# Context attention in a transformer block: one output tile, the regrouping of score blocks and the order of two half weighings are moved

## The chip, the cores and the metric

The kernel runs on 1 core of one Trainium2 chip. The metric is device time in microseconds (us) of one execution. A core has five engines with instruction streams of their own: TensorE (PE, matmuls; PEld its weight loads), VectorE (DVE), ScalarE (ACT), GpSimd (POOL) and SyncE (SP, which here issues almost all DMAs). Each executes its stream in the order in which it was written; semaphores tie them together.

## What is computed

One transformer block in float32 on x of 2 x 1024 x 256 with a context of 2 x 154 x 192: self attention, context ("cross") attention, and a gated feed-forward part, each behind a layer norm and with a residual.

```python
h = _layernorm(x, ln1_g, ln1_b)
x = _attention(h, h, sa_wq, sa_wk, sa_wv, sa_wo, sa_bo) + x
h = _layernorm(x, ln2_g, ln2_b)
x = _attention(h, cond_emb, ca_wq, ca_wk, ca_wv, ca_wo, ca_bo) + x
h = _layernorm(x, ln3_g, ln3_b)
p = h @ ff_w1 + ff_b1
a, gate = (p[..., :D_FF], p[..., D_FF:])
h = a * jax.nn.gelu(gate, approximate=False) @ ff_w2 + ff_b2
return h + x
```

Both attentions have 16 heads of 64; softmax runs over 1024 keys in the first and over 154 in the second.

## The kernel before

The order of all instructions is written out by hand (`manual_schedule`): every engine gets its instructions in the order in which the Python code emits them.

The work is cut into 16 units (2 batches x 8 pairs of heads). Three loops follow each other: self attention (to about 700 us), context attention (48 groups `c`, about 700 to 903 us), and the gated part (steps `k`, from there to the end). In context attention a unit has three groups, of 3, 3 and 2 tiles of 128 queries; group `c` belongs to unit `ui = c // 3` and has the place `n = c % 3` in it.

A unit `u` of context attention passes these stations:

- its query weights are loaded by DMA (L134, `ca_wq`) at group 3(u-2)+1, its queries are projected (`cross_queries`, `pq_ca`, two banks of PSUM) at group 3(u-1), and ScalarE copies them out (L381, `q_ca`);
- at groups 3u to 3u+2 its scores are made (`cross_first`, `sc`, L828), VectorE takes their maximum (`neg`, L834), ScalarE the exponents (L845), VectorE the reciprocals (`rden`, L853) and GpSimd scales (L856);
- two groups later each group is transposed by VectorE (`cross_turn`, L872) into one of three rings `pT_ca`; the last of a unit at group 3u+4;
- `cross_regroup` (L889) copies the blocks from the ring with eight DMAs of 128 KB into one buffer `pTc["pairs"]` (named `wf` in the trace), so that two blocks stand on the partitions that one matmul wants. There is one such buffer for all units: the blocks of unit u may be written only when those of unit u-1 have been read;
- at group 3u+7 `cross_weigh` runs `cross_values` (`poc`, L908) for two halves: half 0 in two banks of the pool `sum_tile` (two banks in all) and half 1 in two banks of the pool `mm_tile` (two banks in all). VectorE copies the four results to `o_ca` (L922); in the gated part ScalarE takes two of the four;
- `out_piece` (L471, `py`) multiplies by the output weights, and VectorE adds the result to x (L478).

Every second unit's values (`context_values`, `pv_ca`, L788) are projected at place 1 of an even unit; their weights (L123, `ca_wv`) are loaded one unit before at place 2. The values are spread over partitions by two DMAs (L800) and four more (L805), which stand in the list `later`. Each group ends with `cross_regroup(c)` and then two entries of `later`; ff weights (L968, L971) and the output weights `ca_wo` (L1287) stand in that list too.

At place 1 of a unit the code runs, in this order: one step of the next layer norm (`side`, through `run_work(0, 1, ...)`), one output tile in a `sum_tile` bank, the values, one output tile in an `mm_tile` bank (`run_work(1, 0)`), the pending additions to x (`flush(adds)`), and `cross_weigh`. The last four output tiles of self attention are put in the list at group 5; two run there, and two at group 7. A step of the layer norm runs only when the tiles that it reads have been added.

In the gated part step `k` counts on as c = 48 + k. Units 14 and 15 are weighed there, at k = 1 and k = 5. `gate_first` takes an `mm_tile` bank (`pa`) and two of another pool; `gate_second` ends with `Gelu` on it (L1066).

Of the kernel before, what the change touches and what calls it, by code (L numbers as in the profile page):

```python
# [18 lines left out]
def tile_transformer_block(ctx: ExitStack, tc: tile.TileContext, a: dict, out: bass.AP):  # L19
# [11 lines left out]
    HP = NPAIR // NQ  # L31
# [182 lines left out]
    hT, vs, qk, oT = {}, {}, {}, {}  # L214
# [347 lines left out]
    def run(piece):  # L562
        done = piece()
        if done is not None:
            (adds if getattr(done, "adds", False) else stores).append(done)

    def flush(queue):
        for fn in queue:
            fn()
        queue.clear()  # L570

    def run_work(n, n_side, bank=None, n_sum=0):

        while n > 0 and work:
            n -= work[0].banks
            run(work.pop(0))
        for _ in range(min(n_side, len(side))):  # L580
            needs_bank, needs, fn = side[0]
            if needs_bank and not bank and n <= 0 or not added.issuperset(needs):
                break
            if needs_bank and not bank:
                n -= 1
            spare["bank"] = bank or mm_tile
            run(fn)
            side.pop(0)
        for i in range(min(max(n, 0) + n_sum, len(outs))):
            spare["out"] = mm_tile if i < n else sum_tile  # L590
            run(outs.pop(0))
# [139 lines left out]
    CG = [(t, min(TG, NT - t)) for t in range(0, NT, TG)]  # L731
# [145 lines left out]

    def cross_regroup(c):

        ui, n = divmod(c - len(CG) - 2, len(CG))  # L880
        if n != 0 or not 0 <= ui < NU:
            return
        for a2 in range(2):
            for a4 in range(P // KB):
                half, e = divmod(a4, 2)
                own = slice(a4 * KB, (a4 + 1) * KB)
                src = slice((2 * half + a2) * KB, (2 * half + a2 + 1) * KB)
                blocks = pTc["ring"][src, ui % 3, :2 * NM].rearrange("p (m e) j q -> p m e (j q)", e=2)
                nc.sync.dma_start(  # L889
                    out=pTc["pairs"][own, a2].rearrange("p m j q -> p m (j q)"), in_=blocks[:, :, e])  # L890

    def cross_values(ui, a2):

        b, pr = units[ui]
        v, v0 = vs["ca", b, pr // 2], pr % 2 * P
        if a2 == 0 and pr % HP == 0:
            oT["ca", b, pr // HP] = pt_.tile([P, HP, S], F32, tag="oT", name=f"o_ca{b}_{pr}")  # L900
        quarters = (a2, 2 + a2)
        po = {a4: (mm_tile if a2 else sum_tile)(f"poc_{ui}_{a4}") for a4 in quarters}
        for m in range(NM + 1):
            for a4 in quarters:
                r0 = a4 // 2 * QG
                r = slice(r0, r0 + QG)
                for j in range(2):
                    nc.tensor.matmul(  # L908
                        po[a4][j * DH:(j + 1) * DH, :NT * KB],
                        lhsT=v[r, m + a2 * (m == NM), v0 + j * DH:v0 + (j + 1) * DH],  # L910
                        rhs=pTc["pairs"][r, a2, m, j] if m < NM else
                        pTc["ring"][r, ui % 3, NB - 1, j, :],
                        start=(m == 0), stop=(m == NM),
                        tile_position=(r0, j * DH),
                    )
        dst = oT["ca", b, pr // HP][:, pr % HP, :].rearrange(
            "p (t a q) -> p t a q", a=P // KB, q=KB)

        def store():
            for a4 in quarters:  # L920
                copy = nc.scalar.copy if pools and a4 // 2 else nc.vector.tensor_copy
                copy(dst[:, :, a4, :], po[a4][:, :NT * KB].rearrange("p (t q) -> p t q", q=KB))  # L922

        return store
# [12 lines left out]
    def cross_drain(c):  # L937

        n = c - 2
        if 0 <= n < CA:  # L940
            cross_turn(n)

    def cross_weigh(c):

        ui, n = divmod(c - 2 * len(CG) - 1, len(CG))
        if n == 0 and 0 <= ui < NU:
            for part in range(2):
                run(lambda: cross_values(ui, part))
            flush(stores)

# [4 lines left out]
    wsum, wh, ub, psum, pools = {}, {}, {}, {}, {}  # L955
# [156 lines left out]
    with tc.manual_schedule():  # L1112
# [59 lines left out]
        for p in range(SA):  # L1172
# [19 lines left out]
            ui, n = divmod(p, 2 * SH)  # L1192
# [8 lines left out]
            if hg == LAG:  # L1201
# [5 lines left out]
                if n == SH + LAG and ui in (0, 1, NU - 1):  # L1207

                    pr = {0: 2, 1: 4, NU - 1: 6}[ui]
# [3 lines left out]
        for c in range(CA):  # L1213
            if c == 1:
                pTc["ring"] = pt_.tile(
                    [P, 2 * NK, QH // 2], F32, tag="pT", name="pT_ca"
                ).rearrange("p a b -> p (a b)")[:, :3 * 2 * NB * NT * KB].rearrange(
                    "p (u n j q) -> p u n j q", u=3, n=NB, j=2)
            if c == SH + 1:
                out_pieces("sa", B - 1, NQ - 1, out_order("sa"))  # L1220
            if c == SH + 1:

                w1, w2, parts = hold_gated()
                add_biases("ca", 0)
                others = later[:] + [lambda: None] * (len(parts) - len(later))
                later[:] = [fn for pair in zip(parts, others) for fn in pair] + others[len(parts):]
            ui, n = divmod(c, len(CG))
            nxt = units[ui + 1] if ui + 1 < NU else None
            if n == 0:
                cross_beside(ui)  # L1230
            elif n == 1 and 1 <= ui < NU - 2:
                load_weights("ca", units[ui + 2][1], "q")
            elif n == 2 and nxt and ui:
                load_weights("ca", nxt[1], "v")
            flush(adds)
            then = cross_first(c)
            if c < 2:
                reciprocals(SA - 2 + c)
            flush(stores)
            if c == 1:  # L1240
                turn_group(SA - 2, 0)
                turn_group(SA - 2, 1)
                scale_rows(SA - 1, 0, 4)
            flush(lates)
            lates.append(then())
            if c == 0:
                join(SA - 1)
                turn_group(SA - 3, 1)
            if c == 2:
                turn_group(SA - 1, 0)  # L1250
                turn_group(SA - 1, 1)
            cross_drain(c)
            if c == 0:
                run(lambda: self_values(2 * NU - 2, 1))
            elif c == 1:
                run(lambda: cross_queries(*nxt))
            elif c == 2:
                run(lambda: cross_queries(*units[2], bank=sum_tile))
            elif c == 3:
                run(lambda: self_values(2 * NU - 1, 0))  # L1260
            elif c == 4:
                run(lambda: self_values(2 * NU - 1, 1))
            elif n == 0 and ui:
                if nxt:
                    run(lambda: cross_queries(*nxt))
                else:
                    run_work(2, 0)
                run_work(0, 1)
            elif n == 1:

                spare["turned"] = True
                run_work(0, 1, sum_tile if outs else None)
                flush(stores)
                run_work(0, 0, n_sum=1)
                if ui % 2 == 0:
                    run(lambda: context_values(*units[ui]))
                run_work(1, 0)
                flush(adds)
                flush(stores)
                cross_weigh(c)  # L1280
            elif n == 2:
                run_work(0, 1, sum_tile if ui == HP + 1 else None)
                if c == SH + 1:
                    run_work(2, 0)
                elif ui == HP:
                    wo["ca"] = const.tile([P, NPAIR, D], F32, tag="wo", name="ca_wo")
                    later[:0] = [lambda i=i: nc.sync.dma_start(  # L1287
                        out=wo["ca"][:, i, :], in_=w["ca_wo"][i * P:(i + 1) * P, :])
                        for i in range(NPAIR)]
            cross_regroup(c)  # L1290
            for _ in range(min(2, len(later))):
                later.pop(0)()
            if c == CA - 16:
                weighted = [fn for n in range(4) for fn in weight_sums(n)]
            if CA - 16 <= c < CA - 4:
                weighted.pop(0)()
            elif c >= CA - 3:
                for n in {CA - 3: (4,), CA - 2: (5, 6), CA - 1: (7,)}[c]:
                    weight_sums(n)[0]()
            if c == CA - 5:  # L1300
                token_sums(0)
# [7 lines left out]
        for k in range(2 * FU):  # L1309
            c = CA + k  # L1310
# [59 lines left out]
```

## Time and profile before

| | |
|---|---|
| runs, median (lowest to highest) | 1085.54 us (1083.54 to 1085.69), 3 runs |
| profiled execution, its time | 1084.96 us |
| its span | 1083.2 us |
| context attention's 16 weighings (`poc`, L908) | first 736.0 us, last 924.5 us |
| regrouping transfers (L889) | 128, 128 KB each |
| granted TensorE clock | 1.00 in all stretches from 715 us on |

The span is the time between the first and the last instruction of the program. "Idle before" is the idle time of an engine just before an instruction, with what ended it behind the arrow. In the order of time, rows of equal instructions are merged: the first column is the start, the second how long they took together, and `x8` their number; `SPq` is SyncE's queue of issues. TensorE's records count each float32 matmul twice, so one weighing of both halves has 48. In the stretches' sums the columns are length, busy time of PE, PEld, DVE, ACT and POOL, granted clock, busy share of DMA, and GB/s.

### The profile page before, as it was taken

To read this page: it belongs to the slowest core of one execution; us is meant where nothing else is said; L and a number is where in the kernel's file an instruction comes from. 1 tells how busy PE (TensorE), PEld (TensorE's weight loads), DVE (VectorE), ACT (ScalarE), POOL (GpSimd) and SP (SyncE) were. 2 spreads that over 40 slices of the span, in tenths; PEclk is the share of its full clock that TensorE was granted. 3 is DMA by queue.
4 is the path that set the end of the run, shared out by engine and by line. 5 is a ranking of instruction groups with operands and counts; after the bars stand their busy time and mean duration, and the time that the engine had idled before them with its cause. 6 is when DMAs were issued, how large, how long until landed. Compare 5 with 4: busy or idle time off the path is not lost.

```text
span 1083.2 us, 46388 instructions
## 1 busy us (share of the span) xinstructions
PE 1067.0 (99%) x19156; PEld 703.2 (65%) x19156; DVE 878.7 (81%) x1297; ACT 643.5 (59%) x2062; POOL 727.1 (67%) x1552
## 2 busy tenths in 40 slices
PE   8999999999999999999999999999999999999998
PEld 6556556556565565575665655566776677788887
DVE  5799999998989989999999889968877887654442
ACT  5766666777667657666776776656555554242321
POOL 2677777777777777677777777776756785475321
PEclk9999999999999999999999999999999999999999
DMA  3222122112111121111111101136765545000000
GB/s 91 68 70 52 39 48 53 43 43 50 32 43 34 30 50 38 34 43 34 33 42 25 43 14 38 29 79 150 191 157 125 119 107 118 1 10 15 11 14 30
DMA packets 104724, 60.81 MB, mean 56 GB/s; under 512 B 32378, under 2 KB 95298, under 8 KB 104514
## 3 DMA queue, kind: packets, MB, share of 16 engines
q1 hardware_dynamic: 103138, 57.07, 22.2%
q8 instruction: 151, 2.47, 1.0%
q10 hardware_dynamic: 1376, 0.79, 0.2%
q14 instruction: 59, 0.48, 0.1%
HBM read 27.91 MB, written 2.10 MB: 28 GB/s over the span
## 4 chain that ended last, share of the span: by engine, by line
PE 83%; DVE 4%; POOL 4%; DMA 3%; SPq 2%; ACT 2%; issue 1%; POOLq 0%; DVEq 0%; ACTq 0%
PE po L549 18%; PE s L497 17%; PE py_sa L471 5%; PE pf L1095 5%; PE py_ca L471 5%; PE pk_sa L366 4%; PE pv_sa L397 4%; PE poc L908 4%; PE pq_ca L366 4%; PE pq_sa L366 4%; PE pb L1029 4%; DMA st<-st 3%; PE sc L828 2%; PE pa L1029 2%; PE pc L1029 2%; SPq L518 2%
## 5 line engine op out<-in xcount | busy, mean ns | idle before, releaser
L619 POOL TENSOR_SCALAR p<-p,rd,ee 128x512 f32<-128x512 f32 x512 | 390.4, 768 | 90.8 <-DVE rd L609 87.7
L508 ACT ACTIVATE p<-s,st 128x512 f32<-128x512 f32 x512 | 345.0, 686 | 171.1 <-DVE st L681 163.7
L681 DVE TENSOR_REDUCE st<-s 128x2 f32<-128x1024 f32 x256 | 308.5, 1206 | 56.9 <-issue 19.0
L644 DVE STREAM_TRANSPOSE pT<-p 128x1024 f32<-128x1024 f32 x256 | 302.7, 1219 | 2.4 <-POOL p L619 2.1
L497 PE MATMUL s<-k_sa,q_sa 64*32 64x512 f32 x4096 | 252.8, 591 | 3.3 <-ACT p L508 2.5
L549 PE MATMUL po<-pT,v_sa 64*32 64x256 f32 x8192 | 237.1, 376 | 1.0 <-DVE pT L644 1.0
L549 PEld LDWEIGHTS po<-pT,v_sa 64*32 64x32 f32 x8192 | 172.9, 106 | 76.2 <-issue 31.2
L497 PEld LDWEIGHTS s<-k_sa,q_sa 64*32 64x32 f32 x4096 | 78.4, 106 | 104.6 <-issue 57.6
L845 ACT ACTIVATE p<-sc,neg 128x154 f32<-128x154 f32 x256 | 96.1, 403 | 83.0 <-DVE rden L853 79.3
L856 POOL TENSOR_SCALAR p<-p,rden 128x154 f32<-128x154 f32 x256 | 96.8, 398 | 56.7 <-DVE rden L853 56.5
L508 ACT ACTIVATION_READ_ACCUMULATOR p<-s,st 128x1 f32 x512 | 103.9, 203 | 0.0
L526 POOL TENSOR_TENSOR dd<-st 128x8 f32<-128x8 f32 x128 | 25.6, 200 | 74.9 <-DMA st<-st 73.0
L397 PEld LDWEIGHTS pv_sa<-sa_wv,hT_ln 64*128 64x128 f32 x1024 | 58.5, 188 | 14.2 <-issue 8.4
L397 PE MATMUL pv_sa<-sa_wv,hT_ln 64*128 64x128 f32 x1024 | 61.8, 275 | 0.0
L471 PE MATMUL py_ca<-ca_wo,o_ca 128*128 128x256 f32 x256 | 60.0, 382 | 0.5 <-DVE o_ca L922 0.5
L366 PE MATMUL pq_ca<-hT_ln,ca_wq 64*64 64x512 f32 (+1 forms) x544 | 60.1, 590 | 0.0
L471 PE MATMUL py_sa<-sa_wo,o_sa 128*128 128x256 f32 x256 | 59.7, 385 | 0.2 <-ACT v_sa L406 0.2
L471 PEld LDWEIGHTS py_sa<-sa_wo,o_sa 128*128 128x128 f32 x256 | 47.3, 190 | 18.2 <-issue 6.9
L834 DVE TENSOR_REDUCE neg<-sc 128x6 f32<-128x924 f32 (+1 forms) x48 | 47.9, 998 | 13.7 <-PE sc L828 13.3
L366 PE MATMUL pq_sa<-hT_ln,sa_wq 64*32 64x512 f32 (+1 forms) x976 | 56.6, 586 | 0.0
L366 PE MATMUL pk_sa<-hT_ln,sa_wk 64*32 64x512 f32 x960 | 56.2, 590 | 0.3 <-ACT q_sa L381 0.3
L845 ACT ACTIVATION_READ_ACCUMULATOR p<-sc,neg 128x1 f32 x256 | 56.1, 219 | 0.0
(121 smaller groups left out, 1418.9 us busy)
## 6 DMA issues: line engine op xcount, KB each, us to landing
wf<-pT_ca SPq DMA_DIRECT2D x128, 128.0 KB
st<-st SPq DMA_DIRECT2D x512, 1.0 KB
v_sa<-v_sa SPq DMA_DIRECT2D x32, 256.0 KB
sa_wq<-in_L_xattn_sa_wq_dram SPq DMA_DIRECT2D x32, 128.0 KB
sa_wk<-in_L_xattn_sa_wk_dram SPq DMA_DIRECT2D x32, 128.0 KB
sa_wv<-in_L_xattn_sa_wv_dram SPq DMA_DIRECT2D x32, 128.0 KB
ca_wq<-in_L_xattn_ca_wq_dram SPq DMA_DIRECT2D x32, 128.0 KB
wf<-in_L_xattn_ff_w_dram SPq DMA_DIRECT2D x12, 256.0 KB
```

The lines of the kernel that those rows point to most:

```text
L366: nc.tensor.matmul(pq[r][f:f + m, at:at + n], lhsT=wt[own, c, f:f + m], rhs=h[own, c, t0:t0 + n], start=(c == 0), stop=(c == NH - 1), tile ...
L397: nc.tensor.matmul(pv[r][:, i * P:(i + 1) * P], lhsT=h[own, c, i * P:(i + 1) * P], rhs=wt[own, c, :], start=(c == 0), stop=(c == NH - 1), ...
L471: nc.tensor.matmul(py[:, e * D:(e + 1) * D], lhsT=o[:, i, (t + e) * P:(t + e + 1) * P], rhs=wo[kind][:, g * HP + i, :], start=(i == 0), st ...
L497: nc.tensor.matmul(sc[a4 * KB:(a4 + 1) * KB, j, :], lhsT=q[r, c:c + KB], rhs=k[r, h * HB:(h + 1) * HB], start=True, stop=True, tile_positi ...
L508: nc.scalar.activation(pr[:, j, :], sc[:, j, :], AF.Exp, bias=st[:, 0, 0, i, j:j + 1], accum_out=st[:, 0, 1, i, j:j + 1],)
L549: nc.tensor.matmul(po[a2][d:d + KB, :QH // 2], lhsT=v[r, t, e, d:d + KB], rhs=pT[r, d // DH * NK + n, :], start=(t == 0 and e == 0), stop= ...
L619: nc.gpsimd.tensor_scalar(pr[:, j, :], pr[:, j, :], own["rd"][:, c:c + 1], own["ee"][:, 0, c:c + 1], op0=ALU.mult, op1=ALU.mult,)
L644: nc.vector.transpose(halves[h][:, :, c:c + KB], slots[p]["p"][i].rearrange("p j (n k) -> p (j n) k", k=KB))
L681: nc.vector.tensor_reduce(st[:, 0, 0, i, :], sc[i], AX.X, ALU.max, negate=True)
L845: nc.scalar.activation(pr_[:, j, i, :T], sc[:, j, i * T:(i + 1) * T], AF.Exp, bias=neg[:, j, i:i + 1], accum_out=den[:, j, i:i + 1],)
L856: nc.gpsimd.tensor_scalar(pr_[:, j, i, :T], pr_[:, j, i, :T], rden[:, j, i:i + 1], 1.0, op0=ALU.mult, op1=ALU.mult,)
L1029: nc.tensor.matmul(into[:, :BT], lhsT=lhs, rhs=wh[pair][i], start=first, stop=True, skip_group_check=True)
```

## The change

Four edits:

- `cross_regroup` runs for unit u at group 3u+4 instead of 3u+5, except for unit 0, which stays at group 5. At group 3u+4 it stands behind the weighing of unit u-1 and ahead of that group's two entries of `later`. For units 14 and 15 this is group 46 and step k = 1.
- At group 7 the second output tile of place 1 (`run_work(1, 0)`) is left out. It is the last entry of the list, and is run at group 10 as the tile in the `sum_tile` bank. At group 10 one more step of the layer norm runs behind the additions.
- In the gated part (`pools` is filled there) half 1 of a weighing comes before half 0.
- The tile for a pair's outputs is made when it is first needed, whichever half comes first.

```diff
     def cross_regroup(c):

-        ui, n = divmod(c - len(CG) - 2, len(CG))
+        ui, n = divmod(c - len(CG) - (2 if c < 2 * len(CG) else 1), len(CG))
...
-        if a2 == 0 and pr % HP == 0:
+        if ("ca", b, pr // HP) not in oT:
             oT["ca", b, pr // HP] = pt_.tile([P, HP, S], F32, tag="oT", name=f"o_ca{b}_{pr}")
...
         if n == 0 and 0 <= ui < NU:
-            for part in range(2):
+            for part in (1, 0) if pools else (0, 1):
                 run(lambda: cross_values(ui, part))
             flush(stores)
...
                 run_work(0, 0, n_sum=1)
                 if ui % 2 == 0:
                     run(lambda: context_values(*units[ui]))
-                run_work(1, 0)
+                run_work(c > 2 * len(CG) + 1, 0)
                 flush(adds)
+                if c == 3 * len(CG) + 1:
+                    run_work(0, 1, sum_tile)
                 flush(stores)
                 cross_weigh(c)
```

## The prediction

> **What bounds the kernel now.** I read first the page's busy shares and its chain of waits, then TensorE's waits from 740 to 930 us (context attention and the join to the gated part), then the orders of time of TensorE, VectorE and SyncE's queue in that stretch, and the stretches' sums.
>
> ```profile
> PE 1067.0 (99%) x19156; PEld 703.2 (65%) x19156; DVE 878.7 (81%) x1297; ACT 643.5 (59%) x2062; POOL 727.1 (67%) x1552
> ...
> PE 83%; DVE 4%; POOL 4%; DMA 3%; SPq 2%; ACT 2%; issue 1%; POOLq 0%; DVEq 0%; ACTq 0%
> ```
>
> TensorE sets the time; only what ends or lengthens one of its waits counts. The change touches groups 7 to 47 and the first six steps of the gated part. TensorE's waits there:
>
> ```profile
> PE poc L908 <- ACT q_ca L381: 1.1, 1, 1.1
> PE poc L908 <- DVE o_ca L922: 0.7, 1, 0.7
> PE py_ca L471 <- DVE o_ca L922: 0.5, 1, 0.5
> PE pa L1029 <- DVE o_ca L922: 0.5, 1, 0.5
> ```
>
> The first stands at 746.82 (group 10, unit 1), the second at 900.86 (group 46, unit 13), the last two behind poc of units 15 and 14. The names mislead in two of them: by the updates of the DMA semaphores in the trace, the last of unit 1's eight regrouping transfers lands at 746.72, and that of unit 13's at 900.72, each 0.1 us before TensorE goes on.
>
> SyncE's queue is the second thing to see: it issues in the order written, and an entry that waits holds all behind it (before unit 15's blocks its queue stood 6.77 us, 905.40 to 912.15, on a transposition). Groups 13 to 17:
>
> ```profile
> 759.91 1.16 SPq L800 DMA_DIRECT2D v_ca<-v_ca  x2
> 761.16 3.10 SPq L805 DMA_DIRECT2D v_ca<-ends  x4
> 764.36 6.04 SPq L889 DMA_DIRECT2D wf<-pT_ca  x8
> 770.43 1.07 SPq L968 DMA_DIRECT2D wf<-in_L_xattn_ff_w_dram  x2
> 771.55 1.36 SPq L134 DMA_DIRECT2D ca_wq<-in_L_xattn_ca_wq_dram  x2
> 772.96 0.60 SPq L968 DMA_DIRECT2D wf<-in_L_xattn_ff_w_dram  x1
> 773.60 0.43 SPq L123 DMA_DIRECT2D ca_wv<-in_L_xattn_ca_wv_dram  x1
> 774.30 6.14 SPq L889 DMA_DIRECT2D wf<-pT_ca  x8
> ```
>
> There is no gap over 14 us, and what is behind is needed at once: the second ca_wq of this stretch lands at 777.23, and its projection pq_ca starts at 777.13. The stretches' sums show why such loads take 4.3 us here and 2.2 us later: DMA is at 0.77 and 0.73 busy before 810, at 0.56 after.
>
> ```profile
> 743.00:780.00 37.00, 35.92 (x483) 25.88 (x478) 32.23 (x75) 22.22 (x105) 28.34 (x75) 1.00 0.77 189
> 780.00:810.00 30.00, 30.00 (x377) 22.76 (x370) 23.18 (x49) 19.51 (x93) 18.28 (x52) 1.00 0.73 178
> 810.00:860.00 50.00, 49.76 (x650) 34.91 (x649) 38.80 (x86) 28.49 (x136) 33.33 (x90) 1.00 0.56 130
> ```
>
> **Blocks regrouped a group sooner.** The same eight transfers are issued per unit; only their place in SyncE's queue moves. They cannot start before poc of the unit before has read the old blocks: units 4, 8, 10 and 12 started 1.12 to 1.15 us after the start of that poc (774.30 after 773.18, 824.64 after 823.52, 849.40 after 848.25, 877.20 after 876.08), already waiting for it. So for even units the new place brings no earlier start; it puts ca_wv behind them. For odd units the six value moves (v_ca) stood ahead and now stand behind.
>
> Gain: unit 13. It started at 892.32 behind value moves; now 1.12 after poc at 889.27, 890.4. Eight issues (mean of thirteen units from the queue's rows: 5.85 us) and 1.8 us of landing end at 898.1 instead of 900.7, before the second half of poc wants them (about 899.2). poc to next scores took 3.97 us here (897.81 to 901.78) against 2.64 at unit 12 (889.27 to 891.91): **-1.3 us**, bounds -0.7 (the named wait alone) and -1.3.
>
> Loss: where value moves could start before poc was read, SyncE worked; now it idles until poc, then issues eight, then six, then the weights. The six cost 3.75 us in quiet (811.04 to 814.76).
> - Group 18's ca_wq: unit 3's blocks at 760.86 + 1.12 = 761.98, + 5.85 + 0.1 + 3.75 = 771.7 for the first ff weight, against 770.43: 1.25 late. The landing had at most 0.1 us to spare: **+1.15**, bounds 0.4 (shortest rows, 5.27 and 3.7) and 2.07 (761.98 less 759.91, if all take as long as before).
> - Group 24's: 786.65 + 1.12 + 9.7 = 797.5 against 795.86: 1.6 late; 802.57 was already its projection's start: **+1.6**, bounds 0.75 and 2.09.
> - Group 12's: unit 1's blocks wait for poc of unit 0, which reads them by 736.6 (next part); 5.7 + 3.75 + four ca_wo issues 2.1 end at 748.2 instead of 747.02: 1.2 late, and pq_ca already waited for its half at 751.44 (issued next at 751.58): **+1.2**, bounds 0 (if poc is not held) and 2.0.
> - Later ca_wq loads (groups 30, 36, 42) end 1 us or more before use without ff weights in the queue: 0. ca_wv, now behind eight issues: at groups 25, 31 and 43 it is issued 6.5 to 7.1 us and lands 8.7 to 9.3 after the release, wanted at 9.0 to 9.4; at group 13, 757.0 + 2.2 to 3.2 against 758.17 + 1.2. I take **+0.3** for all, bounds 0 and 3.
>
> One rule bears on this. The Trainium skill, "DMA: Bandwidth & Descriptors", section "Anatomy of one DMA — SWDGE (gpsimd) path", fits a transfer as 2.0 us and its bytes at 436 GB/s, 2.3 us for ca_wq's 128 KB, and says that waits on semaphores are made by the issuing sequencer. The second half the 6.77 us row confirms; by the first, an estimate, groups 18 and 24 lose nothing and the whole would come out 0.3 us faster. The rows of this stretch say 4.3 us, and the row decides. The rule is fitted on another queue's path.
>
> **The output tile moved from group 7 to 10.** No work is added: eight py_sa records (1.73 us) and one VectorE addition (0.63) move, and the layer norm's third step (two statistics 1.05, off 0.29, GpSimd 0.9 + 1.08) follows them from group 8 to 10, as its inputs need the tile. In group 7 the removed matmuls hid something:
>
> ```profile
> 734.73 0.48 DVE L785 MEMSET v_ca<- 128x512 f32 x1
> 735.14 0.63 DVE L478 TENSOR_TENSOR x<-py_sa,x 128x512 f32<-128x512 f32 x1
> ```
>
> poc's second bank is the one this addition empties. poc could start at 734.19 (now 736.01) but after four records waits until 735.82; group 37 shows it: four at 862.73, the next at 863.77, named DVE x. Next scores at 735.82 + 44/48 of 2.64 = 738.24 against 738.65: -0.4, not -1.8. In group 10 the query eviction (now 746.15) ends about 745.6, so the 1.08 wait goes, but the addition, behind neg, rden and transpositions from 744.0 on (1.05, 0.17, 0.86), ends at 746.6 and holds the second bank: scores 11 at 749.05, the transpose ph_ln at 749.8 against 749.27: +0.5, bounds -1.5 (no bank wait) and +1.5. This lies beside, not on top of, group 12's late ca_wq: the projection waits for that anyway. So **0** here; without that cover +0.5.
>
> **Gated part's banks first.** The same 48 records per unit in another order, twice. For unit 14, pa at 914.12 waited 0.51 for a main bank's copy; these banks now empty under the other half of poc: **-0.5**. They must be free earlier: Gelu frees one at 910.50, poc starts at 910.79, so nothing is added (bounds 0 and +0.3). For unit 15 py_ca needs all four copies, whose last stays where it was: 0. Unit 15's blocks start up to 0.9 later and land by 920.4, wanted at 922: 0.
>
> **Sum** against the profiled execution (span 1083.2, time 1084.96): -1.3 + 1.15 + 1.6 + 1.2 + 0.3 - 0.5 = +2.45, 1087.4. The median of the runs, 1085.54, lies 0.58 higher, so **1088.0**.
>
> **Rivals.**
> - *Loads keep ahead* (faster). If ca_wq lands in 2.2 us as at 820.94, nothing is late at groups 12, 18 and 24, the 1.1 of group 10 goes, and 1.3 and 0.5 with it: -2.9, **1082.6**. For: after 810 they do. Against: 4.3 us in the rows of 771 to 798, beside ff weights. It decides from 1 us shorter landings.
> - *Values are late too* (slower still). ca_wv comes 0.9 us late at groups 13, 19, 25 and 31, on top: +3.6 less the 0.3 counted, **1091.3**. For: 5.48 and 4.51 us landings at 773.60 and 799.09. Against: 2.2 us in quiet, and each wait at a ca_wq gives ca_wv time.
> - *It does little*: the blocks wait for poc wherever they stand, value moves run in SyncE's gaps, and only the banks' 0.5 is seen: **1085.0**. For: the even units. Against: unit 13's 892.32.
>
> **How the numbers follow.** Main case 0.55, its own range 1086.3 to 1090.0; loads ahead 0.22; values late 0.15; little 0.08. A measurement of this kernel tells about 0.2% (2.17 us) from no change. Slower takes 0.38 of the main case and 0.15; within takes 0.17 of it, 0.05 and 0.08; faster the other 0.17. The range 1083.3 to 1091.0 leaves out most of the faster case and the upper part of values late.
>
> **What would show it.** SyncE's queue idle before L889 of odd units and v_ca after it; TensorE waiting at pq_ca of groups 12, 18 and 24; poc of unit 0 held after four records; no wait at poc of unit 13 nor at pa behind unit 14. Wrong: pq_ca without a gap there (then faster), or the 1.1 us wait still in group 10.

## The result, and the profile after

| | before | after |
|---|---|---|
| median (lowest to highest), 9 runs each, interleaved | 1083.54 us (1082.49 to 1085.69) | 1089.15 us (1086.06 to 1091.07) |
| profiled execution, its time / its span | 1084.96 / 1083.2 | 1086.06 / 1084.3 |

The ratio after to before is **1.0042**, 95% interval 1.0029 to 1.0055: slower by more than the 0.2% that can be told from no change. Note that the profile of after comes from the fastest of its nine executions; a second profile of the same kernel (e8 below) has a span of 1089.0.

TensorE's busy time and the make-up of the chain, from the page of after:

```profile
PE 1068.5 (99%) x19156; PEld 704.1 (65%) x19156; DVE 878.5 (81%) x1297; ACT 644.7 (59%) x2062; POOL 730.6 (67%) x1552
...
PE 86%; DMA 3%; DVE 3%; SPq 3%; POOL 3%; ACT 1%; issue 1%; POOLq 0%; DVEq 0%; ACTq 0%
```

As many matmuls as before; TensorE still sets the time. Its waits from 720 to 932 us in after (total, times, longest):

```profile
PE pv_ca L788 <- DMA ca_wv<-in_L_xattn_ca_wv_dram: 1.6, 2, 1.1
PE poc L908 <- DVE x L478: 1.5, 3, 0.9
PE pq_ca L366 <- DMA ca_wq<-in_L_xattn_ca_wq_dram: 1.3, 2, 0.7
```

The four waits of before that the prediction shows are gone: the 1.1 of group 10, the 0.7 of unit 13, the two of 0.5 in the gated part. In their place stand waits for weights: ca_wv for the values (the largest), ca_wq for the queries, and an output tile's addition that holds a bank of poc (0.89 in group 7 and 0.20 in group 10; the third, 0.4 in group 37, was there before). SyncE's queue, groups 12 to 17 of after:

```profile
757.19 1.33 SPq L134 DMA_DIRECT2D ca_wq<-in_L_xattn_ca_wq_dram  x2
761.80 5.29 SPq L889 DMA_DIRECT2D wf<-pT_ca  x8
767.18 1.66 SPq L800 DMA_DIRECT2D v_ca<-v_ca  x2
768.94 2.48 SPq L805 DMA_DIRECT2D v_ca<-ends  x4
771.46 1.05 SPq L968 DMA_DIRECT2D wf<-in_L_xattn_ff_w_dram  x2
772.56 1.39 SPq L134 DMA_DIRECT2D ca_wq<-in_L_xattn_ca_wq_dram  x2
774.12 6.25 SPq L889 DMA_DIRECT2D wf<-pT_ca  x8
780.42 0.58 SPq L968 DMA_DIRECT2D wf<-in_L_xattn_ff_w_dram  x1
781.05 0.45 SPq L123 DMA_DIRECT2D ca_wv<-in_L_xattn_ca_wv_dram  x1
```

Two things are to be seen against the rows of before. The queue now stands idle from 758.5 to 761.8: the first L889 waits until poc has read the old blocks, and the six value moves, which ran in that gap, stand behind it. And ca_wv, formerly issued at 773.60 ahead of the even unit's blocks, is issued at 781.05 behind them. TensorE's order of time shows who pays (idle time in brackets):

```profile
750.77 4.04 PE L366 MATMUL pq_ca<-hT_ln,ca_wq 64*64 64x512 f32 x32 [0.63 <-DMA ca_wq<-in_L_xattn_ca_wq_dram]
...
784.83 1.10 PE L788 MATMUL pv_ca<-ca_wv,ctxT 96*128 96x256 f32 x4 [0.51 <-DMA ca_wv<-in_L_xattn_ca_wv_dram]
...
804.35 3.85 PE L366 MATMUL pq_ca<-hT_ln,ca_wq 64*64 64x512 f32 x29 [0.70 <-DMA ca_wq<-in_L_xattn_ca_wq_dram]
...
812.48 1.10 PE L788 MATMUL pv_ca<-ca_wv,ctxT 96*128 96x256 f32 x4 [1.14 <-DMA ca_wv<-in_L_xattn_ca_wv_dram]
```

Group 10, which got the output tile, and unit 13's weighing in group 46, in after:

```profile
742.50 1.99 PE L471 MATMUL py_sa<-sa_wo,o_sa 128*128 128x256 f32 x8
744.42 0.65 PE L908 MATMUL poc<-wf,v_ca 64*64 64x256 f32 x4
745.28 0.86 PE L908 MATMUL poc<-wf,v_ca 64*64 64x256 f32 x10 [0.20 <-DVE x L478]
...
901.63 1.04 PE L908 MATMUL poc<-wf,v_ca 64*64 64x256 f32 x16
902.49 0.61 PE L908 MATMUL poc<-pT_ca,v_ca 64*64 64x256 f32 x8
902.92 1.04 PE L908 MATMUL poc<-wf,v_ca 64*64 64x256 f32 x16
903.78 0.61 PE L908 MATMUL poc<-pT_ca,v_ca 64*64 64x256 f32 x8
904.22 0.70 PE L828 MATMUL sc<-kT,q_ca 64*64 64x154 f32 x16
```

In group 10 four records run, then poc's second bank waits for the tile's addition. Unit 13's poc now runs without a break, 2.59 us to the next scores.

**How the shifts are worked out.** The same matmul is looked up in two profiles; each start is counted from the first score matmul of group 6 (726.27 in before, 724.68 in after), because the upstream part, which the change doesn't touch, differs by up to 1.8 us among the profiles. The difference is how late TensorE is by then. At the end after stands at +2.69; less the 1.59 by which its reference point is earlier, that is 1.10, the difference of the spans. This table is worked out from the traces that way, in us:

| by the end of | after | e8, after again | e1 blocks | e2 tile | e3 banks | e4 queue order | e5 values ahead | e6 unit 13 | e7 and weights |
|---|---|---|---|---|---|---|---|---|---|
| poc 1, group 10 | +0.85 | +0.85 | +0.02 | +0.85 | 0 | +0.85 | +0.85 | 0 | 0 |
| pq_ca, group 12 | +1.16 | +3.96 | +4.50 | +1.39 | +0.22 | +1.24 | +0.90 | +0.54 | -0.66 |
| pv_ca, group 13 | +1.40 | +3.96 | +4.50 | +1.39 | +0.22 | +1.23 | +1.85 | +0.54 | -0.66 |
| pq_ca, group 18 | +1.78 | +4.74 | +5.70 | +1.27 | +0.21 | +1.55 | +1.74 | +0.53 | +0.31 |
| pv_ca, group 19 | +2.53 | +5.82 | +7.05 | +1.27 | +0.21 | +1.55 | +3.92 | +0.53 | +0.31 |
| pq_ca, group 24 | +3.85 | +7.77 | +8.46 | +1.47 | +0.03 | +1.33 | +3.70 | +1.17 | +0.22 |
| pv_ca, group 25 | +5.22 | +8.91 | +9.22 | +1.47 | +0.03 | +1.33 | +5.31 | +1.17 | +0.22 |
| poc 12, group 43 | +5.40 | +9.49 | +9.67 | +1.50 | +0.06 | +1.33 | +6.54 | +0.95 | -0.01 |
| poc 13, group 46 | +3.61 | +7.70 | +7.89 | +1.05 | -0.19 | -0.46 | +4.75 | -0.84 | -1.79 |
| poc 15, gated part | +3.03 | +7.12 | +7.89 | +1.05 | -0.77 | -1.04 | +4.17 | -1.42 | -2.38 |
| the end | +2.69 | +6.78 | +7.92 | +1.07 | -1.13 | -1.39 | +3.83 | -1.76 | -2.72 |

### The profile page after: what moved, and what is told of

It is laid out like the page before. It is cut to its first block, busy times and chain, and to the rows that moved or that the text cites. A ratio compares the mean times of both kernels' runs of the same rounds, so it can differ in the third digit from the quotient of the medians.

```text
span 1084.3 us, 46385 instructions
## 1 busy us (share of the span) xinstructions
PE 1068.5 (99%) x19156; PEld 704.1 (65%) x19156; DVE 878.5 (81%) x1297; ACT 644.7 (59%) x2062; POOL 730.6 (67%) x1552
## 4 chain that ended last, share of the span: by engine, by line
PE 86%; DMA 3%; DVE 3%; SPq 3%; POOL 3%; ACT 1%; issue 1%; POOLq 0%; DVEq 0%; ACTq 0%
PE po L549 19%; PE s L497 19%; PE pf L1095 5%; PE py_sa L471 5%; PE pv_sa L397 5%; PE py_ca L471 5%; PE pq_sa L366 4%; PE pk_sa L366 4%; PE poc L908 4%; PE pb L1029 4%; PE pq_ca L366 3%; PE pa L1029 2%; PE pc L1029 2%; PE sc L828 2%; DMA st<-st 1%; SPq L518 1%
```

## The experiments

The theory: TensorE loses to weights that come late because the regrouping transfers hold SyncE's queue. Its rivals: the output tile or the order of the banks costs the time. All were run beside the kernel before, e1 to e4 together on one chip (its median 1085.25), e5 to e8 (1085.44) and e9 to e11 (1085.77) likewise. The clock column counts the runs whose mean granted TensorE clock was under 1 (8 of 57 for the kernel before). A mean of 0.999 can come from the program's end alone: e2's profiled execution has it, and its clock falls only behind the last matmul, from 1083.1 us on. Runs at 0.998 or less are 4 of 57 for the kernel before, none for e2 and e3, 3 for e5 and 2 for e10; the other counts stay.

| kernel | median us | ratio to before, 95% | clock under 1 |
|---|---|---|---|
| e1, blocks sooner alone | 1092.21 | 1.0069 (1.0057 to 1.0082) | 5 of 5 |
| e2, output tile alone | 1085.63 | 1.0005 (0.9996 to 1.0015) | 1 of 11 |
| e3, banks alone | 1084.55 | 0.9991 (0.9982 to 1.0000) | 1 of 11 |
| e4, changed kernel, loads and value moves ahead of the blocks | 1082.57 | 0.9975 (0.9964 to 0.9985) | 0 of 8 |
| e5, changed kernel, value moves alone ahead | 1087.32 | 1.0016 (1.0004 to 1.0028) | 5 of 12 |
| e6, before with banks and unit 13's blocks sooner | 1082.46 | 0.9973 (0.9964 to 0.9982) | 0 of 9 |
| e7, e6 with one ca_wq a group sooner | 1082.18 | 0.9971 (0.9959 to 0.9983) | 0 of 6 |
| e8, the changed kernel again | 1090.95 | 1.0056 (1.0041 to 1.0071) | 4 of 5 |
| e9, the changed kernel with one ca_wq a group sooner | 1092.29 | 1.0051 (1.0036 to 1.0067) | 4 of 6 |
| e10, e1 with TensorE's wait filled | 1092.26 | 1.0060 (1.0047 to 1.0072) | 3 of 6 |
| e11, e1 again | 1093.76 | 1.0072 (1.0059 to 1.0085) | 5 of 5 |

### Each part alone

**e1**: the kernel before with the regrouping a group sooner and nothing else.

```diff
-        ui, n = divmod(c - len(CG) - 2, len(CG))
+        ui, n = divmod(c - len(CG) - (2 if c < 2 * len(CG) else 1), len(CG))
```

> The regrouping a group sooner alone. Queue theory (weights stand behind blocks that wait for poc): 3 to 5 us slower than before; SyncE idle ahead of the blocks of odd units, TensorE waiting at pq_ca of groups 12, 18 and 24 and at pv_ca of groups 19 and 25, each 0.4 to 1.5 us, unit 13's poc 1.3 to 1.8 us shorter. Tile theory (the output tile moved to group 10 is what costs): within 1 us of before or faster, no new wait in groups 12 to 25.

Measured: 1.0069. This part alone loses more than the whole change, and its 7.0 us are more than the 3 to 5 expected: group 12 alone is +4.50. Group 12 in e1, first SyncE's queue, then TensorE:

```profile
735.91 6.44 SPq L889 DMA_DIRECT2D wf<-pT_ca  x8
742.44 1.18 SPq L800 DMA_DIRECT2D v_ca<-v_ca  x2
743.72 2.48 SPq L805 DMA_DIRECT2D v_ca<-ends  x4
746.24 3.04 SPq L1287 DMA_DIRECT2D ca_wo<-in_L_xattn_ca_wo_dram  x4
749.33 1.39 SPq L134 DMA_DIRECT2D ca_wq<-in_L_xattn_ca_wq_dram  x2
```

```profile
745.61 1.35 PE L908 MATMUL poc<-wf,v_ca 64*64 64x256 f32 x14 [1.18 <-ACT q_ca L381]
...
752.68 5.40 PE L366 MATMUL pq_ca<-hT_ln,ca_wq 64*64 64x512 f32 x29 [3.01 <-DMA ca_wq<-in_L_xattn_ca_wq_dram]
```

ca_wq goes out 24.3 us after group 6's first scores (749.33 - 725.04) against 20.8 in before (747.06 - 726.27), and its projection stands 3.01 us. The wait in group 10 is still there, 1.18 us, so the sooner blocks do nothing for it; it was the query eviction's. The first of the two evictions (L381) ends at 745.55 in e1, 0.06 us before TensorE goes on, and at 746.77 in before, 0.05 us before it does: there the blocks' landing at 746.72 only fell on the same moment.

**e2**: the output tile alone.

```diff
-                run_work(1, 0)
+                run_work(c > 2 * len(CG) + 1, 0)
                 flush(adds)
+                if c == 3 * len(CG) + 1:
+                    run_work(0, 1, sum_tile)
```

> The output tile moved from group 7 to group 10 alone. Queue theory: within 0.7 us of before, since the wait that goes in group 10 is given back at the second bank of poc in groups 7 and 10. Tile theory: 3 us slower or more. In both, poc of unit 0 stops after four records, for about 1.1 us.

Measured: 1.0005, no difference that can be told; its profile ends 1.07 later. In group 7 poc starts 1.73 us sooner but stands after four records for the addition and ends only 0.21 sooner. In group 10 it loses 1.06, so +0.85 stays: 1.73 of matmuls come in, the wait of 1.08 goes, and the hold behind four records takes the remaining 0.41. The tile alone is about even; it is not what makes the change slow.

It matters a little in company. The sooner start of poc 0 releases unit 1's blocks 0.6 us sooner: they start 10.3 us after the reference point in after (734.96 - 724.68) and 10.9 in e1 (735.91 - 725.04). The issue of group 12's ca_wq differs by more, 24.3 us in e1, 22.4 in after (747.04 - 724.68) and 22.7 in e8 (748.09 - 725.35), but most of that is the four ca_wo issues ahead of it, 3.04 us in e1's profile and 1.96 in after's. In e10 below, which has e1's order, ca_wq goes out at 23.3.

**e3**: the banks alone.

```diff
-            for part in range(2):
+            for part in (1, 0) if pools else (0, 1):
```

> The main banks' half first in the gated part alone. 0.9 us faster: the wait of pa behind unit 14 (0.51) goes, and of the wait of py_ca behind unit 15 some 0.4, as its first matmuls read unit 14. If the order of the halves cost something (Gelu frees the bank too late): 0 to 0.5 us slower, with a wait at poc of unit 14.

Measured: 0.9991, its interval just reaches 1; the profile ends 1.13 sooner. Of that, 0.58 comes at pa behind unit 14's poc, and 0.36 behind unit 15's, where the prediction had put 0. In after:

```profile
926.73 3.50 PE L471 MATMUL py_ca<-ca_wo,o_ca 128*128 128x256 f32 x14
```

py_ca follows poc without a gap, and it starts 0.53 us before the last of unit 15's copies ends (927.26). Its first records read unit 14's outputs; what they waited for was a bank, not unit 15's copies.

### The order in SyncE's queue

**e4**: the changed kernel, but at place 1 the value moves and ca_wv (taken from place 2) go ahead of the blocks, except at group 43, whose blocks (unit 13's) stay first.

```diff
-            elif n == 2 and nxt and ui:
+            elif n == 2 and nxt and ui == 1:
...
-            cross_regroup(c)
+            behind = c < 2 * len(CG) or c == CA - 5
+            if behind:
+                cross_regroup(c)
...
+            if n == 1 and c > 2 * len(CG) and nxt:
+                load_weights("ca", nxt[1], "v")
+            if not behind:
+                cross_regroup(c)
```

> The changed kernel with the values' transfers and the value weights put ahead of the blocks again, but for unit 13. Queue theory: all waits at pq_ca of groups 18 and 24 and at pv_ca of groups 13, 19 and 25 go or fall to those of before; 1 to 2.5 us faster than before, 5 us faster than the changed kernel. If the blocks' earlier place loads the DMA engines at a worse time, whatever the order, it stays 2 us or more slower than before.

Measured: 0.9975, 2.7 us faster than before. The whole loss and more is gone, with the tile and the banks kept. The code still names the sooner groups, but SyncE's queue has the order of before again for all units but 13 (and the same order as e6 below). Groups 13 to 17 of e4, which can be laid beside the rows of before and of after:

```profile
759.41 1.16 SPq L800 DMA_DIRECT2D v_ca<-v_ca  x2
760.65 3.00 SPq L805 DMA_DIRECT2D v_ca<-ends  x4
763.75 6.58 SPq L889 DMA_DIRECT2D wf<-pT_ca  x8
770.38 1.09 SPq L968 DMA_DIRECT2D wf<-in_L_xattn_ff_w_dram  x2
771.51 1.36 SPq L134 DMA_DIRECT2D ca_wq<-in_L_xattn_ca_wq_dram  x2
772.92 0.60 SPq L968 DMA_DIRECT2D wf<-in_L_xattn_ff_w_dram  x1
773.57 1.58 SPq L123 DMA_DIRECT2D ca_wv<-in_L_xattn_ca_wv_dram  x1
```

TensorE's waits from 720 to 932 in e4:

```profile
PE poc L908 <- DVE x L478: 1.5, 3, 0.9
PE pq_ca L366 <- DMA ca_wq<-in_L_xattn_ca_wq_dram: 0.5, 1, 0.5
```

No wait for ca_wv is left, and of ca_wq's one of 0.5; the waits for the tile's addition are the same 1.5 as in after. From group 12 to 43 TensorE's shift stays between +1.23 and +1.55, the tile's, and unit 13 then takes 1.79 back. e4 and the changed kernel differ in the queue's order alone, so this settles the main question: the order of the queue is the loss. Since the blocks are back in their old place, e4 can't by itself exclude the expectation's rival, that blocks sooner load the DMA engines at a worse time. The rows of after speak against it: the loads for groups 18 and 24 were issued late there but landed faster than in before (3.5 and 2.6 us against 4.3 and 4.2).

**e5**: only the value moves ahead again; ca_wv still behind.

```diff
+            values = n == 1 and ui % 2 == 0 and 2 * len(CG) < c < CA - 5
+            if not values:
+                cross_regroup(c)
...
+            if values:
+                cross_regroup(c)
```

> The changed kernel with only the values' transfers (L800, L805) ahead of the blocks again, the value weights (ca_wv) still behind. Theory now: the waits at pq_ca of groups 18 and 24 belong to the values' transfers and go; those at pv_ca of groups 19 and 25 belong to ca_wv and stay, and grow, since TensorE arrives sooner: 0.8 to 1.6 us each. 1 to 3 us slower than the order with both ahead; about the time of before or up to 1.5 us slower. Rival (one wait is only exchanged for the next, and the slot is bound by what DMA carries): as slow as the changed kernel.

Measured: 1.0016, 1.9 us slower than before and so a little over the 1.5 expected. TensorE's largest waits in e5:

```profile
PE pv_ca L788 <- DMA ca_wv<-in_L_xattn_ca_wv_dram: 4.0, 4, 1.9
PE poc L908 <- DVE x L478: 1.5, 3, 0.9
```

This splits the loss by its two weights (the longest wait, 1.9 us, is over the 1.6 expected). ca_wq's waits are all gone: the value moves, pushed behind the blocks, were what made ca_wq late. ca_wv's waits stay, and at 4.0 are larger than after's 1.6: a projection that no longer waits for ca_wq brings the values' turn sooner. So the two losses stand in for each other in part, and removing one shows more of the other.

### What is worth keeping

**e6**: the kernel before with e3's banks and the sooner regrouping for unit 13 alone.

```diff
-        ui, n = divmod(c - len(CG) - 2, len(CG))
-        if n != 0 or not 0 <= ui < NU:
+        ui, n = divmod(c - len(CG) - (1 if c == CA - 5 else 2), len(CG))
+        if c == CA - 4 or n != 0 or not 0 <= ui < NU:
```

> The kernel before with the main banks' half first in the gated part, and the blocks of unit 13 alone a group sooner; the output tile stays in group 7. The two gains add up (1.1 and 1.8 us): 2.9 us faster than before, 1.0 us faster than the order with both ahead, which keeps the moved tile. If the earlier blocks of unit 13 only move the wait to the next bank: 1.1 us faster.

Measured: 0.9973. One unit of fifteen gives all the gain that the sooner regrouping has, 1.79 at group 46 against the profile of before, and nothing of its loss. That profile is an unlucky one at this place: from poc of unit 13 to the next output tile (py_ca) before takes 5.01 us, while e2 and e3, with the same blocks' place, take 4.55 and 4.76. All kernels with sooner blocks take 3.22 or 3.23. So the gain is 1.3 to 1.8 us.

**e7**: e6 with ca_wq of unit 5 loaded at group 9 instead of 10, for the projection of group 12.

```diff
+                if ui == len(CG):
+                    load_weights("ca", units[ui + 2][1], "q")
-            elif n == 1 and 1 <= ui < NU - 2:
+            elif n == 1 and 1 <= ui < NU - 2 and ui != len(CG):
```

> As the run with unit 13's blocks sooner, and unit 5's query weights loaded ahead of two of the output weights' transfers, at group 9 instead of 10. The wait of pq_ca in group 12 (0.4 to 0.9 us) goes: 0.4 to 0.9 us faster than that run. If DMA's load and not the place in the queue sets the landing: the same time.

Measured: 0.9971. e6's wait of 0.4 for ca_wq is gone from e7's profile, and that profile ends 0.96 sooner than e6's, but the medians differ by 0.28 us and the intervals nearly coincide: whether the sooner load is worth anything isn't shown. Both beat the kernel before and the changed one.

**e8**: the changed kernel unaltered, for a second profile.

> The changed kernel once more, for a second profile: counted from group 6 its profiled execution lost 2.7 us while the medians stand 5 us apart. If landings behind the ff weights vary from one execution to the next, this profile shows other sizes at pq_ca of groups 12, 18 and 24 and pv_ca of 19 and 25, between 2 and 6 us in sum; if the rest lies elsewhere (self attention, the gated part's end), they are the same to 0.2 us.

Measured: 1.0056, span 1089.0. Group 12's projection in e8, and two stretches around it (length, busy of PE, PEld, DVE, ACT, POOL, granted clock, DMA, GB/s):

```profile
752.94 5.34 PE L366 MATMUL pq_ca<-hT_ln,ca_wq 64*64 64x512 f32 x32 [2.13 <-DMA ca_wq<-in_L_xattn_ca_wq_dram]
```

```profile
752.00:754.00 2.00, 1.06 (x5) 0.80 (x9) 1.97 (x6) 0.25 (x1) 1.85 (x6) 0.64 0.93 206
754.00:756.00 2.00, 2.00 (x16) 1.13 (x12) 2.00 (x6) 2.00 (x12) 1.72 (x5) 0.50 0.93 202
756.00:758.00 2.00, 2.00 (x24) 1.36 (x20) 0.11 (x1) 0.08 (x1) 1.38 (x4) 1.00 0.85 216
```

Two things make the 2.80 by which e8 is later than after at this point. The wait is 1.50 longer: by the updates of the DMA semaphores ca_wq's two loads landed 4.0 and 3.4 us after their issue, against 2.9 and 2.4 in after. And the projection itself takes 5.34 us where it took 4.04 (the first of after's rows above): behind the wait TensorE's granted clock stood at 0.50. The banks' and unit 13's terms are the same in both.

### The clock behind a wait

e1's profile has the same 0.50 behind its wait of 3.01 us, and its projection takes 5.40. Two kernels and a repeat look into this.

**e9**: the changed kernel with e7's edit, which takes away the wait at group 12.

> The changed kernel with one load moved: ca_wq of unit 5 goes out at group 9 instead of 10, so it stands ahead of unit 1's blocks' followers and group 12's projection need not wait for it. If group 12's late ca_wq (0.63 us of wait in one profile, 2.13 and a granted clock of 0.5 behind it in the other) is what lifts the changed kernel's usual time above its fastest execution, no wait at pq_ca of group 12, granted clock 1.00 all through context attention, and a ratio of 1.002 to 1.0035, with a narrower spread than 1086 to 1091. If the later weights (groups 18, 19, 24, 25) make the difference, the ratio stays at 1.004 to 1.0055.

Measured: 1.0051, no gain. The first theory falls: the wait for ca_wq at group 12 is gone (+0.87 there, the tile's), but the next load takes its place, and the clock falls behind that one. TensorE in e9, then the stretches:

```profile
760.12 1.10 PE L788 MATMUL pv_ca<-ca_wv,ctxT 96*128 96x256 f32 x4 [1.67 <-DMA ca_wv<-in_L_xattn_ca_wv_dram]
761.06 3.54 PE L471 MATMUL py_ca<-ca_wo,o_ca 128*128 128x256 f32 x8
```

```profile
760.00:762.00 2.00, 1.88 (x7) 1.63 (x8) 0.67 (x2) 0.72 (x2) 1.92 (x4) 0.78 0.70 215
762.00:764.00 2.00, 2.00 (x7) 1.52 (x5) 0.00 (x0) 0.01 (x1) 0.01 (x1) 0.50 0.28 78
```

Eight py records take 3.54 us where they take 1.89 at full clock, 1.65 more. Of e9's six runs the four with a clock under 1 took 1092.2 to 1094.5 us, the two at full clock 1088.5 and 1089.0. In other kernels the clock doesn't part the runs so: e8's run at full clock took 1090.95 us, in the middle of its other four (1090.82 to 1092.81).

**e10**: e1 with four matmuls ahead of group 12's projection, whose results are overwritten by it, so that TensorE works through most of the wait.

```diff
+        if (b, pr) == units[5]:
+            h = hT["ca", b]
+            for i in range(4):
+                nc.tensor.matmul(pq[0][:, :D], lhsT=h[:, 0, :P], rhs=h[:, 0, :D], start=True, stop=True)
```

> Blocks sooner alone, with four matmuls (128x128 by 128x256, results overwritten) put ahead of the projection of group 12, so that TensorE works for some 1.7 us of the 3.0 us in which it waits for ca_wq there. If the half granted clock behind that wait (0.50 in 754 to 756 us, the projection 5.4 us instead of 3.6 to 4.0) comes from the idle time, the clock stays at 1.00, the projection takes 3.6 to 4.1 us, and the kernel is 1.2 to 1.7 us faster than without the four matmuls although it does more. If the projection is slow for another reason (transfers beside it), it stays at 5.4 us and the time stays the same.

**e11**: e1 unaltered, beside it.

> Blocks sooner alone, unaltered, to stand beside the one with the wait filled on the same chip: ratio 1.0057 to 1.008, a wait of 2.5 to 3.5 us at pq_ca of group 12 and a granted clock of 0.5 for about 3 us behind it.

Measured: 1.0060 for e10 and 1.0072 for e11, whose intervals overlap. In e10's profile:

```profile
749.49 1.99 PE L741 MATMUL pq_ca<-hT_ln 128*128 128x256 f32 x8
751.68 3.96 PE L366 MATMUL pq_ca<-hT_ln,ca_wq 64*64 64x512 f32 x29 [0.20 <-DMA ca_wq<-in_L_xattn_ca_wq_dram]
```

With 1.99 us of extra work the wait shrinks to 0.20, the clock stays at 1.00 to the end of context attention, and the projection takes 3.96 us instead of e1's 5.40. Three of its six runs still show a clock under 1, one of them at 0.999; that later waits brought it is likely but not shown. Its three runs at full clock took 1090.4, 1092.2 and 1094.2 us, the others 1090.9 to 1094.5, so the clock isn't what sets them apart. e11 misses its own expectation in part: behind a wait of 2.57 at group 12 its projection takes 4.01 at full clock, and the clock falls at group 18 instead, in a projection with waits of 0.39 and 1.59. The projection of group 12, and the stretch at group 18 (granted clock 0.55):

```profile
752.61 4.01 PE L366 MATMUL pq_ca<-hT_ln,ca_wq 64*64 64x512 f32 x30 [2.57 <-DMA ca_wq<-in_L_xattn_ca_wq_dram]
...
782.00:784.00 2.00, 1.20 (x8) 0.60 (x12) 1.26 (x4) 1.83 (x10) 2.00 (x6) 0.55 0.70 161
```

In the profiles each fall inside the program comes at a wait, but not each wait brings one. That the idle time causes it fits e10's one profile and the counts of all runs (none of 23 in e4, e6 and e7, whose longest wait from 720 us on is 0.9 us; ten of ten in e1 and e11), but what it is worth in time isn't proved: the medians of e10 and e11 differ by 1.5 us, as expected, but their intervals overlap.

## Why the prediction was right

It said 1088.0 and slower; the median was 1089.15, inside its range. The mechanism of its likeliest case happened: loads late behind blocks that wait for poc, TensorE standing at the projections, unit 13 and the banks gaining. The size is in part luck. The forecast was 2.5 us more than before's 1085.54; measured beside each other, after's median is 5.6 us above before's, which was 1083.54 in these runs. And in the sum errors of both signs cancel, as the terms show against the shifts of the two profiles of the changed kernel:

| term | predicted | after | e8 |
|---|---|---|---|
| groups 10 and 12: tile and ca_wq together | +1.2 | +1.16 | +3.96 |
| group 18, ca_wq | +1.15 | +0.38 | +0.78 |
| group 24, ca_wq | +1.6 | +1.32 | +1.95 |
| ca_wv, all groups | +0.3 | +2.54 | +2.80 |
| unit 13's blocks, group 46 | -1.3 | -1.79 | -1.79 |
| banks, unit 14 | -0.5 | -0.58 | -0.58 |
| banks, unit 15, and the rest | 0 | -0.34 | -0.34 |
| sum | +2.45 | +2.69 | +6.78 |

- **ca_wv was the mis-sized term.** It was put at 0.3 and came to 2.5. It was worked out as issued 6.5 to 7.1 us after the release by poc, landing 8.7 to 9.3 after, for groups 25, 31 and 43; group 19 was not worked out. At group 19 the issue ended 7.4 us after the release (781.5 after 774.1), the landing took 3.2 us more and not 2.2, and pv_ca stood 0.51. At group 25 the queue was late itself: the blocks were released at 800.64 (1.12 after poc at 799.52), but the queue was still busy with the late ca_wq until 802.21, so the issue of ca_wv ended 9.3 us after the release and pv_ca stood 1.14. Each was priced as if the queue were free at the release, and with ca_wq late it wasn't. The rival "values are late too" named groups 13, 19, 25 and 31 at 0.9 each; after lost 0.24 at group 13, 0.75 at 19, 1.37 at 25 and 0.18 from there to group 43. So this term came nearer to the rival's 3.6 than to the 0.3, and what happened is a mixture of the two cases.
- **Groups 18 and 24.** The issue was late as worked out: 1.2 at group 18 (1.02 by the clock, TensorE being 0.19 ahead by it) where 1.25 was said. But the second load landed in 3.5 us there and 2.6 at group 24, against 4.3 and 4.2 in before, so less was lost at group 18 than +1.15. At group 24 eight issues and six moves took 11.0 us (788.71 to 799.68) where 9.7 was said, so there the two errors nearly cancel, by luck. The fit of the Trainium skill ("DMA: Bandwidth & Descriptors", section "Anatomy of one DMA — SWDGE (gpsimd) path") gave 2.3 us and no loss; the rows lie between it and the 4.3, and the loss was there.
- **Group 12 and the tile.** That the tile's cost hides behind the late ca_wq held in after, +1.16 against +1.2; of it +0.85 is there before group 12 and is the tile's. Alone it is larger than the +0.5 given for the case without cover: e2 shows +1.06 at group 10, less the 0.21 that group 7 gains (-0.4 was said). What was missed is how far this term moves: in e8 it is 3.96, above the bounds' 2.0, as the wait was longer and the clock fell behind it. **No term of the sum held a slower clock after a wait**; that is worth 1.3 us in e8 and 1.65 in e9.
- **Unit 13** gave 0.5 more than its bound in this pair of profiles; against e2 and e3 (see e6) it is 1.3 and 1.5. The step read the old duration up to the first scores (3.97 us). In before the last poc records stand behind that row, at 901.96, and the scores run until py_ca at 902.82; measured up to py_ca the old stretch was 5.01 (902.82 - 897.81), the new 3.22 (904.85 - 901.63).
- **The wait of group 10.** The prediction said that its name, the query eviction, misleads, and named the blocks' landing. By e1 the name was right. No term of the sum rests on it.
- **Banks.** Unit 14 as predicted. "py_ca needs all four copies" was wrong for unit 15, as e3 shows.
- **The profile and the median.** The sum met the profiled execution, +2.69 against +2.45, but that is luck, as that execution is the fastest of nine: group 12's wait was short in it and the clock did not fall. The median lies 3.1 us above it, where the prediction added 0.58. Landings and the clock explain e8; one of the nine runs shows a clock under 1, and how the other eight came to differ by up to 5 us can't be told without their traces.

The DMA share shows the landings' other side, from the stretches' sums of after (length, busy of PE, PEld, DVE, ACT, POOL, clock, DMA, GB/s):

```profile
743.00:780.00 37.00, 36.16 (x457) 25.28 (x460) 31.94 (x77) 20.18 (x95) 27.13 (x71) 1.00 0.68 169
780.00:810.00 30.00, 28.79 (x366) 20.49 (x359) 20.81 (x44) 18.22 (x84) 16.72 (x47) 1.00 0.64 157
```

DMA is at 0.68 and 0.64 busy against 0.77 and 0.73 before: fewer bytes move in these stretches. The ca_wq of groups 18 and 24 land sooner there, but not every load does: the two that follow them, issued from 782.51 and 810.47 on, land 3.9 and 3.6 us after their issue (the second half of each), against 3.6 and 2.2 for the same loads in before. From 810 to 860 us DMA is 0.57 busy in after and 0.56 in before, so the share of a stretch alone doesn't tell how long a load takes; the prediction's "show why" was too strong.

## What to carry to other kernels

In a queue that issues in order, a transfer that must wait for a buffer to be read gains nothing from standing earlier; it only takes the time that ready entries behind it would have used. So put loads that can go at once ahead of entries that wait for a release, and move an entry forward only where the profile shows its own start late behind other work (here one unit of fifteen). When one such delay is removed, price the next load again with the queue as it then stands: in e5 and e9 the wait taken away at one weight came back at the next. And a TensorE wait of 2 us or so can cost more than its length, by what the matmuls behind it take at half clock (here up to 1.65 us more).

## What was not expected of the hardware

- Waits of 1.67, 2.13 and 3.01 us were followed by some 3.4 us at a granted clock of 0.5 (e9, e8, e1; in e9 the stretches' 0.78, 0.50 and 0.86 of 2 us each make 0.88 + 2.0 + 0.56), waits of 1.95 (e5), 1.74 and 2.57 (both e11) were not, and in e11 a fall began within a wait of 1.59. Such a fall can cost 1.7 us at most, half its length. The Trainium skill, "TensorE: Matmul & The Clock Gate", section "What's actually happening", has the clock drop to half after at least one idle window of about 3.4 us, on a window that runs freely. The steady window agrees with these runs: by the traces' records of the granted clock each of the four falls lasts 3.41 us, and from its start (753.75 in e1, 752.57 in e8, 761.14 in e9, 782.19 in e11) to the start of the fall behind that program's last matmul it is a whole number of 3.413 us, 99, 99, 97 and 91. That a fall needs 3.4 us of idle time does not agree, since none of these waits was so long. In the 3.41 us before the four falls TensorE stood idle for 2.34, 1.76, 1.67 and 1.37 us in sum. Yet the 1.74 us in e11 (809.51 to 811.25), all within one such window, brought no fall, so the idle time alone doesn't decide either; what else counts isn't shown.
- The same load in the same program landed 2.4 or 3.4 us after its issue in two executions (ca_wq's second half for group 12, after and e8).
- Some loads that were held back landed faster: ca_wq for group 24 in 2.6 us against 4.2 in before, at a DMA share of 0.64 against 0.73 between 780 and 810 us. So a late issue is not always lost in full. That the transfers beside it decide is likely, but no run takes them away.
